# A graph layer on one core: node features as 64-row columns, 16-bit column lists made once, column copies in two of five groups, batch maxima in the other 64 partitions

## The chip, the core and the metric

One core of a Trainium2 chip runs the kernel. Its engines are named as in the profile: PE (matrix), DVE (vector), ACT (scalar), POOL and SP; each takes its instructions in order, and they wait for one another with semaphores. DMA queues are filled by SP, ACT and POOL. The metric is device time in microseconds (us). The kernel before took 3988.75, 3981.80 and 3985.86 us in three runs, a median of 3985.86.

## The reference

`x` holds 12500 nodes of 64 features. There are 412,500 edges (sender `src`, receiver `dst`, 32 edge features), sorted by receiver. Cut to what matters:

```python
h = relu(layernorm(x))
z = concat([h[src], h[dst], edge])                  # 64 + 64 + 32
messages = silu(z @ W1 + b1) @ W2 + b2
logits   = silu(z @ Wa1 + ba1) @ Wa2 + ba2
att      = softmax(logits, axis=0)                  # over all edges
agg      = segment_sum(messages * att, dst)
out      = x + silu(concat([h, agg]) @ Wu1 + bu1) @ Wu2 + bu2
```

The first products split into a part of the sender's node, one of the receiver's and one of the edge, so the parts of the nodes are made once for each node.

## The kernel before, in words

**Tiles.** The nodes are padded to NP = 12544, in 98 blocks of 128. The edges stand in columns of 128; K = 8 columns are a group, and NG = 403 groups make the main loop. A column's first layer is 128 wide: 64 of the message and 64 of the attention logit.

**The node stage** takes the layer norm of `x` in chunks, transposes it (`hT`: two blocks of nodes stacked on 128 partitions, so a node's 64 features are in the lower or in the upper half of a column), and makes two tables in DRAM: `ts_d` with the sender's part (stores L274 on SP's queue) and `tr_d` with the receiver's (stores L310 on ACT's queue). The last store of the stage, L313, puts `hT` itself into DRAM.

**The main loop** (L738) does for each group `load(g + 2)`, `begin(g)` and `end(g)`, with the sums of an earlier group in between:
- `load`: POOL issues one indirect DMA for each column (L533), which gathers 128 rows of `ts_d` into one of seven `gs` buffers; SP loads the window of receivers, the edge features and the receivers' numbers; DVE compares the numbers (L558), and PE multiplies (L562) into the PSUM tile `pe`.
- `begin`: DVE adds `gs` and `pe` (L573), ACT takes the tanh of the sum (L576).
- `end` and after: DVE makes the messages' activations and logits (L586 to L597), PE sums them by node (L646), and DVE adds the sums into the table `sums` (L671, L675).

**The softmax** goes by batches of groups with a running maximum. `put` also notes for each node the maximum of its batch, in the table `stand` (L678), which is laid out like `sums`: 128 partitions, of which 64 belong to one half of the nodes and 64 to the other, and one value repeated over the 64.

**Chosen groups.** Every third group, from 10 to 388, is chosen (127 of 403). In these the eighth column isn't gathered. Instead ACT copies its 128 columns of `hT` one by one into the tile `cols` (L504), each from a place whose number stands in a register (loads L500), and PE multiplies `cols` with the sender's weights (L568). Before that, SP loads the senders' numbers of the column to all partitions (`numbers`, L478), DVE turns them into column numbers with six operations (`places`, L487 to L493), and one more (L567) clears the half of each copied column that belongs to the other node. `burst` spreads the copies over six slots, two in each of the three groups before.

**The end** (L869 to L888). When the last group is summed, 13 tiles of 8 blocks (the last of 2) go through `factor` (ACT, the exponential of a batch's maximum, from `stand` into PSUM, L830), `first` (DVE, L838, and POOL, L843), `silu` (ACT's tanh, L848, and DVE, L849), `second` (PE, 4 matmuls in 8 passes, L856) and `rest` (DVE, L862, and the store of the output by SP, L864). The tiles take the three PSUM buffers of `acts_ps` in turn: `factor(t)` writes buffer t % 3, and the tanh of the same tile overwrites it. The loop's body is `first(t)`, `factor(t + 1)`, `silu(t - 1)`, `second(t - 1)`, `rest(t - 2)`; the engines' queues are then put in an order by a scheduler, except where `pin` keeps the order of the program.

A second path, `general`, is there for inputs whose receivers don't fit the windows. It doesn't run on these inputs.

Of the kernel before, what the change touches and what calls it, by code (L numbers as in the profile page):

```python
# [44 lines left out]
F32 = mybir.dt.float32  # L45
I32 = mybir.dt.int32
AF = mybir.ActivationFunctionType
# [6 lines left out]
P = 128  # L54
# [19 lines left out]
EVERY = 3  # L74
PHASE = 1
SLOTS = (((0, 24), (24, 24)), ((48, 24), (72, 12)), ((84, 24), (108, 20)))
# [4 lines left out]
BIG = 3.0e38  # L81


PARTS = [("pair", 4 * C), ("we", C), ("bias", C), ("wu2h", 2 * D), ("wa2", U), ("bu2", D), ("w_bu", U),
         ("w2b", U), ("wu1a", U), ("wu2", D), ("ba2", 1), ("w_bup", 2 * U), ("bu1", 1)]
# [5 lines left out]
def gnn_kernel(ctx: ExitStack, tc: tile.TileContext, n_edges, x, src, src_row, dst, dst_row, first, edge,  # L91
# [14 lines left out]
    hT_d = dram.tile([2 * D, NB // 2, P], F32, name="hT_d")  # L106
# [19 lines left out]
    w_bu = part["w_bu"][:D + 1]  # L126
# [29 lines left out]
    hT = const.tile([2 * D, NB // 2, P], F32, name="hT")  # L156
# [8 lines left out]
    with tc.tile_pool(name="node1", bufs=1) as node1, \  # L165
# [7 lines left out]
        for c, n in chunks:  # L173
            xc = node.tile([P, CB, D], F32, name="xc", bufs=min(len(chunks), 8))[:, :n, :]
# [138 lines left out]
        pin(nc.scalar.dma_start(hT_d, hT))  # L313
# [6 lines left out]


def node_bias(tc, b, v, work, ps):

    nc = tc.nc
    NB, w_bu = v["NB"], v["w_bu"]
    n = min(4, NB - b)
    hb = work.tile([D + 1, 4, P], F32, name="hb")
    nc.vector.memset(hb[D:, :, :], 1.0)
    for r in range(2):
        nc.sync.dma_start(hb[:D, r:n:2, :], v["hT_d"][r * D:(r + 1) * D, b // 2:(b + n) // 2, :])  # L330
    pb = ps.tile([P, 4, P], F32, name="mt")
    nc.tensor.matmul(pb[:U, :n, :], w_bu, hb[:, :n, :], start=True, stop=True)
    return pb[:U, :n, :]
# [60 lines left out]
def one_pass(tc, n_edges, v):  # L394
# [17 lines left out]
    with ExitStack() as ctx:  # L412
# [5 lines left out]
        stand = keep.tile([P, NH + 2 * W], F32, name="stand")  # L418
# [15 lines left out]
        nc.vector.memset(start[:, 1:2], BIG)  # L434
# [5 lines left out]
        hT = v["hT"].rearrange("d b p -> d (b p)")  # L440
        stack = keep.tile([2 * D, C], F32, name="stack")
        nc.vector.tensor_tensor(stack, v["w_pair"][:, 0, :C], v["w_pair"][:, 0, C:], ALU.add)
        half = keep.tile([P, 1], F32, name="half")
        nc.vector.memset(half[:D], 0.0)
        nc.vector.memset(half[D:], 1.0)
# [10 lines left out]
        with tc.tile_pool(name="work2", bufs=2) as work2, \  # L456
# [3 lines left out]
            pes, gss, lgs, ps_, psums, sps, pps, ees, mts, nums, cols = ({} for _ in range(11))  # L460
# [10 lines left out]

            chosen = {g for g in range(8, NG - 12) if g % EVERY == PHASE}

            def numbers(g):
                if g in chosen:
                    e = (g * K + K - 1) * EP
                    n = nums[g] = small.tile([P, EP], I32, name="num", bufs=2)
                    nc.sync.dma_start(n, bass.AP(tensor=v["src_row"].tensor,  # L478
                                                 offset=v["src_row"][:, e:].offset, ap=[[0, P], [1, EP]]))

            def places(g):
                if g not in chosen:
                    return
                n = nums[g]
                near = small.tile([1, EP], F32, name="near", bufs=1)
                to = small.tile([1, EP], I32, name="to", bufs=2)
                pin(nc.vector.tensor_scalar(to, n[0:1], 1, None, op0=ALU.logical_shift_right))  # L487
                m = NB // 2
                pin(nc.vector.tensor_scalar(near, to, 1.0 / m, 0.5 / m - 0.5, op0=ALU.mult, op1=ALU.add))
                pin(nc.vector.tensor_scalar(near, near, ROUND, None, op0=ALU.add))  # L490
                pin(nc.vector.tensor_scalar(near, near, ROUND, float(1 - m * P), op0=ALU.subtract, op1=ALU.mult))
                pin(nc.vector.scalar_tensor_tensor(to, to, float(P), near, op0=ALU.mult, op1=ALU.add))
                pin(nc.vector.tensor_scalar(n, n, 1, None, op0=ALU.bitwise_and))  # L493
                cols[g] = small.tile([P, EP], F32, name="cols", bufs=2), to

            def columns(g, first, n):
                if g not in chosen:
                    return
                to, at = cols[g]
                _, regs = nc.values_load_multi_w_load_instructions(  # L500
                    at[0:1, first:first + n], engines=[ENG.Activation], min_val=0, max_val=NP // 2 - 1,
                    skip_runtime_bounds_check_because=WHY)
                for i in range(n):
                    pin(nc.scalar.copy(to[:, first + i:first + i + 1], hT[:, bass.ds(regs[i], 1)]))  # L504
# [19 lines left out]
            def load(g):  # L524
# [40 lines left out]
                if g in chosen:  # L565
                    to, _ = cols[g]
                    pin(nc.vector.scalar_tensor_tensor(to, nums[g], half, to, op0=ALU.is_equal, op1=ALU.mult))  # L567
                    pin(nc.tensor.matmul(pe[:, K - 1, :], to, stack, start=False, stop=True))  # L568
# [91 lines left out]
            def put(g, part=None):  # L660

                if g % NQ == 0 and g not in at_lo:
                    registers(g, ENG.DVE, at_lo, base_lo, NH + W)
                    registers(g, ENG.DVE, at_hi, base_hi, NH + W)
                s = batch[g]
                for h, at in enumerate((at_lo, at_hi)):
                    rows, cols = slice(h * U, (h + 1) * U), bass.ds(at[g], W)
                    if part != "stand":
                        pp = pps[g]
                        if g == starts[s]:  # L670
                            pin(nc.vector.scalar_tensor_tensor(sums[rows, cols], sums[rows, cols],  # L671
                                                               scale[rows, s:s + 1], pp[rows],
                                                               op0=ALU.mult, op1=ALU.add))
                        else:
                            pin(nc.vector.tensor_tensor(sums[rows, cols], sums[rows, cols], pp[rows],  # L675
                                                        ALU.add))
                    if part != "sums":
                        pin(nc.vector.tensor_copy(stand[rows, cols],  # L678
                                                  nmax[rows, s + 1:s + 2].to_broadcast([U, W])))
# [8 lines left out]
            def inputs(t):  # L688

                n = P // 2 * NC  # L690
                if t < 8:
                    i = (t // 4 + (NG - 1) // NQ + 1) % 2
                    bs[t], xs[t] = eos[i][:, t % 4 * n:(t % 4 + 1) * n], hT[:, t * n:(t + 1) * n]
# [40 lines left out]

            for g in range(AHEAD):
                load(g)
            done = 0
            for g in range(NG):  # L738
# [9 lines left out]
                if g < 4:  # L748
                    w = -(-(NH + 2 * W) // 4)
                    for k, table in enumerate((sums, stand)):  # L750
                        piece = table[:, g * w:min((g + 1) * w, NH + 2 * W)]
                        pin(nc.scalar.activation(
                            piece, start[:, k:k + 1].to_broadcast([P, piece.shape[1]]), AF.Copy))
# [5 lines left out]
                numbers(g + 7)  # L759
                places(g + 6)  # L760
# [57 lines left out]
            free.append(hT[:, 8 * P // 2 * NC:8 * P // 2 * NC + K * C])  # L818
# [6 lines left out]
            def factor(t):  # L825
                n = width(t)
                if t in (1, 2):
                    acts_ps.append(one_ps.tile([P, 4, P], F32, name=(None, "sp", "mt")[t]).rearrange("p k c -> p (k c)"))
                fac = facs[t] = acts_ps[t % 3][:, :P // 2 * n]
                pin(nc.scalar.activation(fac.rearrange("u (p b) -> u p b", b=n),  # L830
                                         fv[:, :, t * NC:t * NC + n], AF.Exp, bias=last, scale=-1.0))
# [59 lines left out]
def general(tc, n_edges, v, dst):  # L891
# [7 lines left out]
    with ExitStack() as ctx:  # L899
# [11 lines left out]
        dst_sb = keep.tile([EP, T], I32, name="dst_g")  # L911
# [14 lines left out]
        with tc.tile_pool(name="bu_g", bufs=2) as work, \  # L926
                tc.tile_pool(name="bu_g_ps", bufs=2, space=PSUM) as bu_ps:
            for b in range(0, NB, 4):
                n = min(4, NB - b)
                bu = work.tile([U, 4, P], F32, name="bu_g")[:, :n, :]  # L930
                nc.scalar.copy(bu, node_bias(tc, b, v, work, bu_ps))
                nc.sync.dma_start(bu_d[:, b:b + n, :], bu)
# [142 lines left out]
def _laid_out(w):  # L1075
# [17 lines left out]
    part["w_bu"][:D + 1] = np.concatenate([w["Wu1"][:D], w["bu1"][None]])  # L1093
# [47 lines left out]
```

## Time and profile before

| | |
|---|---|
| runs | 3988.75, 3981.80, 3985.86 us |
| profiled execution | 3986.92 us, of which its span is 3985.1 us |
| mean granted clock of PE | 0.64 |
| HBM traffic | 360.42 MB read, 25.72 MB written |

A row of the page's fifth part reads: line, engine, operation, output <- inputs, count, then busy us and mean ns of one, then the engine's idle time just before and what ended most of it. A row of a timeline reads: start in us from the start of the span, us, engine, line, operation, and in brackets the idle time before and its releaser. "x8" in such a row is eight instructions in a row, put together.

### The profile page before, as it was taken

How to read it: one execution, taken by the hardware profiler on the slowest of the kernel's cores; microseconds unless marked ns; L12 is line 12 of the kernel's file. 1: busy time of each engine (PE TensorE's matmuls, PEld its weight loads, DVE VectorE, ACT ScalarE, POOL GpSimd, SP SyncE). 2: the span in 40 equal slices, each digit the busy share in tenths (PEclk: the TensorE clock that was granted, in tenths of full speed). 3: DMA queues.
4: the chain of work that ended last, by engine and by line, in shares of the span. 5: the costliest groups of instructions: out<-in, count | busy, mean ns of one | idle time of the engine just before them, and what ended most of it. 6: DMA issues, size and time to landing. Idle time of an engine off the chain costs nothing. (4 is left out here: it accounts for less than half of the span.)

```text
span 3985.1 us, 80416 instructions
## 1 busy us (share of the span) xinstructions
PE 2332.9 (59%) x11238; PEld 1888.3 (47%) x11238; DVE 3264.8 (82%) x9553; ACT 2173.0 (55%) x17477; POOL 2950.2 (74%) x3122
## 2 busy tenths in 40 slices
PE   6556566666666555555555555555655555555566
PEld 5444444454444444444444444444544444444455
DVE  6888888888888787888878888887878887878787
ACT  3655555555555555555555555555555555555512
POOL 3777777777777777777777777777777777777774
PEclk8766666666666666666666666666666665666666
DMA  8333343333333333333333333333333333333333
GB/s 287 101 99 99 95 110 92 103 99 102 102 92 95 93 85 93 87 92 88 89 94 84 95 93 86 94 84 94 88 91 94 84 95 87 91 95 84 104 105 85
DMA packets 219778, 391.64 MB, mean 98 GB/s; under 512 B 72209, under 2 KB 146898, under 8 KB 206050
## 3 DMA queue, kind: packets, MB, share of 16 engines
q0 software_dynamic: 99104, 203.16, 19.1%
q1 hardware_dynamic: 118754, 173.60, 16.7%
q10 hardware_dynamic: 1376, 9.67, 0.6%
q14 instruction: 452, 3.70, 0.3%
q8 instruction: 92, 1.51, 0.2%
HBM read 360.42 MB, written 25.72 MB: 97 GB/s over the span
## 5 line engine op out<-in xcount | busy, mean ns | idle before, releaser
L533 POOL DMA_INDIRECT gs<-ts_d,src_sb x3097 | 2933.0, 947 | 992.6 <-issue 854.1
L562 PE MATMUL pe<-wins,eo 128*128 128x256 f32 x3224 | 1465.1, 630 | 925.7 <-DVE eo L558 679.6
L504 ACT COPY cols<-hT 128x1 f32 x16256 | 1605.0, 187 | 717.7 <-issue 714.8
L562 PEld LDWEIGHTS pe<-wins,eo 128*128 128x128 f32 x3224 | 970.9, 318 | 1222.7 <-DVE eo L558 769.0
L576 ACT ACTIVATE pe<-gs 128x1024 f32<-128x1024 f32 x403 | 413.7, 1026 | 928.6 <-DVE gs L573 496.8
L573 DVE TENSOR_TENSOR gs<-pe,gs 128x1024 f32<-128x1024 f32 (+1 forms) x403 | 475.4, 1180 | 393.6 <-DMA gs<-ts_d,src_sb 369.2
L640 DVE TENSOR_SCALAR wt<-iota_w,dloc,p 128x40 f32<-128x40 f32 x3224 | 726.1, 321 | 1.8
L646 PE MATMUL sp<-wt,acts 128*65 128x40 f32 x6448 | 628.8, 268 | 6.3 <-DVE wt L640 3.9
L646 PEld LDWEIGHTS sp<-wt,acts 128*65 128x65 f32 x6448 | 589.9, 183 | 16.2 <-DVE wt L640 9.7
L657 PEld LDWEIGHTS mt<-ss,w2u 65*128 65x128 f32 x806 | 203.0, 279 | 336.2 <-issue 173.9
L657 PE MATMUL mt<-ss,w2u 65*128 65x40 f32 x806 | 181.6, 319 | 242.3 <-DVE gm L623 202.0
L616 PE MATMUL mt<-ident,mx 128*128 128x128 f32 x107 | 47.4, 443 | 445.8 <-DVE sums L675 427.2
L594 DVE TENSOR_TENSOR pe<-pe,w_all 128x512 f32<-128x512 f32 x403 | 281.8, 699 | 13.4
L558 DVE TENSOR_SCALAR eo<-dbs,bj 64x256 f32<-64x256 int32 x806 | 277.9, 375 | 18.2 <-DMA dbs<-in_dst_row_dram 9.0
L592 DVE SCALAR_TENSOR_TENSOR pe<-pe,gs 128x512 f32<-128x512 f32 x403 | 280.3, 696 | 10.5
L586 DVE SCALAR_TENSOR_TENSOR acts<-pe,gs 128x512 f32<-128x512 f32 x403 | 277.2, 688 | 12.4 <-ACT pe L576 3.2
L597 DVE TENSOR_REDUCE lg<-pe 128x8 f32<-128x512 f32 x403 | 277.0, 687 | 10.5
L616 PEld LDWEIGHTS mt<-ident,mx 128*128 128x128 f32 x107 | 19.5, 182 | 456.9 <-issue 455.0
L678 DVE COPY stand<-nmax 64x40 f32 x806 | 161.0, 200 | 3.2
L671 DVE SCALAR_TENSOR_TENSOR sums<-sums,scale,mt 64x40 f32 x214 | 54.2, 253 | 89.2 <-PE mt L657 85.0
L675 DVE TENSOR_TENSOR sums<-sums,mt 64x40 f32 x592 | 111.5, 188 | 4.7 <-PE mt L657 0.6
L357 DVE TENSOR_SCALAR bu<-mt,w_all 64x256 f32<-64x256 f32 (+1 forms) x50 | 23.9, 477 | 88.7 <-PE mt L348 88.3
(124 smaller groups left out, 1062.7 us busy)
## 6 DMA issues: line engine op xcount, KB each, us to landing
eo<-in_edge_dram SPq DMA_DIRECT2D x100, 512.0 KB
dbs<-in_dst_row_dram SPq DMA_DIRECT2D x200, 256.0 KB
gs<-ts_d,src_sb POOLq DMA_INDIRECT x3097
wins<-tr_d SPq DMA_DIRECT2D x806, 32.0 KB
num<-in_src_row_dram SPq DMA_DIRECT2D x127, 64.0 KB
ts_d<-ts SPq DMA_DIRECT2D x5, 896.0 KB
tr_d<-tr ACTq DMA_DIRECT2D x5, 896.0 KB
hT_d<-hT ACTq DMA_DIRECT2D x1, 3136.0 KB
```

The source lines that it names most:

```text
L504: pin(nc.scalar.copy(to[:, first + i:first + i + 1], hT[:, bass.ds(regs[i], 1)]))
L533: nc.gpsimd.indirect_dma_start(out=full[:rows, j, :], out_offset=None, in_=ts_d[:, :], in_offset=bass.IndirectOffsetOnAxis(ap=src_full[:ro ...
L558: pin(nc.vector.tensor_scalar(eo[:WR, e], db[:, e], bj[g // NQ % 2 * WR:(g // NQ % 2 + 1) * WR, g, h:h + 1], None, op0=ALU.is_equal))
L562: pin(nc.tensor.matmul(pe[:, 2 * q:2 * q + 2, :], eo[:, q * EP:(q + 1) * EP], win[:, q // 2, :, :], start=True, stop=q < H - 1 or g not in ...
L573: pin(nc.vector.tensor_tensor(gss[g][:, :n, :], pes[g][:, :n, :], gss[g][:, :n, :], ALU.add))
L576: pin(nc.scalar.activation(pes[g], gss[g], AF.Tanh))
L586: pin(nc.vector.scalar_tensor_tensor(acts[g % ACTS][:, :, 0:U], th[:, :, U:C], 1.0, gs[:, :, U:C], op0=ALU.add, op1=ALU.mult))
L592: pin(nc.vector.scalar_tensor_tensor(att, th[:, :, 0:U], 1.0, gs[:, :, 0:U], op0=ALU.add, op1=ALU.mult))
L594: pin(nc.vector.tensor_tensor(att, att, wa2[:EP, None, :].to_broadcast([EP, K, U]), ALU.mult))
L640: pin(nc.vector.tensor_scalar(wt[:, j, :], iota_w[:EP, j // H, :], dloc[:, g * K + j:g * K + j + 1], p[:, k + j:k + j + 1], op0=ALU.is_equ ...
L646: pin(nc.tensor.matmul(sp, acts[g % ACTS][:, j, :], wt[:, j, :], start=j == 0, stop=j == K - 1))
L657: pin(nc.tensor.matmul(pp, w2u.rearrange("s h u -> s (h u)"), sps.pop(g), start=True, stop=True))
```

## The change

- **Chosen groups**: from 10 to 390, those with g % 5 of 0 or 3, 153 of 403. The copies of one chosen group have five slots of 32 or 24 columns, one for each half group, beginning 9 or 10 half groups ahead.
- **One column a node**: the new tile `hS` holds `hT` in its first NP/2 columns. Its other columns hold, on partitions 0 to 63, a copy of the upper half of `hT` (`upper`: four DMAs inside SBUF on SP's queue, 64 x 1568 floats each), so that each node is one column on partitions 0 to 63. `cols` has 64 partitions, the mask of L567 goes, and the matmul contracts over 64 rows (`w_s`). The chunks of `x` are loaded into parts of `hS` first.
- **Lists**: `column_lists` works out the column numbers of all chosen groups at once, 7 DVE operations for each of the two residues, and stores them in DRAM as 16-bit numbers; `listed` loads one line of 128 of them for each chosen group. `numbers` and `places` go, and with them the 127 loads of numbers.
- **Batch maxima**: `stand` is now the other half of `hS`, partitions 64 to 127 and columns from NP/2: 32 rows for each half of the nodes. In `factor`, a matmul with the 0/1 matrix `pick` spreads the two values over 64 partitions each, into PSUM, and the exponential then works in place.
- The store of `hT` in DRAM goes, and with it `node_bias`, which only `general` used.

```diff
-EVERY = 3
-PHASE = 1
-SLOTS = (((0, 24), (24, 24)), ((48, 24), (72, 12)), ((84, 24), (108, 20)))
+EVERY = 5
+LEADS = {0: 9, 3: 10}
+SLOTS = ((0, 32), (32, 24), (56, 24), (80, 24), (104, 24))
+FIRST = 10
...
-        pin(nc.scalar.dma_start(hT_d, hT))
...
-        stand = keep.tile([P, NH + 2 * W], F32, name="stand")
+        stand = v["hS"][D:, NH:]
...
+        w_s = v["w_pair"][:D, 0, :C]
+        pick = keep.tile([P, P], F32, name="pick")
+        nc.vector.memset(pick, 0.0)
+        for h in range(2):
+            nc.vector.memset(pick[D + R * h:D + R * h + 1, h * U:(h + 1) * U], 1.0)
...
-            chosen = {g for g in range(8, NG - 12) if g % EVERY == PHASE}
+            chosen = [g for g in range(FIRST, NG - 12) if g % EVERY in LEADS]
+            of_phase = {r: [g for g in chosen if g % EVERY == r] for r in LEADS}
...
+            def column_lists():
+                m = NB // 2
+                for i, (r, gs) in enumerate(of_phase.items()):
+                    n, e = len(gs), (gs[0] * K + K - 1) * EP
+                    num = small.tile([P, EP], I32, name="num", bufs=2)[:n]
+                    nc.sync.dma_start(num, bass.AP(tensor=v["src_row"].tensor, ...
...
+                    pin(nc.vector.scalar_tensor_tensor(column, num, float(NH), near, op0=ALU.mult, op1=ALU.add))
+                    nc.sync.dma_start(v["list_d"][i, :n, :], column)
+
+            def upper(k, n):
+                w = -(-NH // n)
+                a, b = k * w, min((k + 1) * w, NH)
+                nc.sync.dma_start(hS[:D, NH + a:NH + b], hS[D:, a:b])
+
+            def listed(g):
                 if g in chosen:
...
+                    to = lists[g] = small.tile([1, EP], U16, name="listed", bufs=3)
+                    nc.sync.dma_start(to, v["list_d"][list(LEADS).index(g % EVERY),
+                                                      (g - of_phase[g % EVERY][0]) // EVERY][None, :])
...
             def columns(g, first, n):
...
+                if first == 0:
+                    cols[g] = small.tile([D, EP], F32, name="cols", bufs=2)
...
-                    pin(nc.scalar.copy(to[:, first + i:first + i + 1], hT[:, bass.ds(regs[i], 1)]))
+                    pin(nc.scalar.copy(cols[g][:, first + i:first + i + 1], hS[:D, bass.ds(regs[i], 1)]))
...
             def burst(g, k):
-                for i in range(EVERY):
-                    columns(g + 3 + i, *SLOTS[EVERY - 1 - i][k])
+                for c in range(g, g + 7):
+                    if c in chosen and 0 <= 2 * g + k - (2 * c - LEADS[c % EVERY]) < len(SLOTS):
+                        columns(c, *SLOTS[2 * g + k - (2 * c - LEADS[c % EVERY])])
...
                 if g in chosen:
-                    to, _ = cols[g]
-                    pin(nc.vector.scalar_tensor_tensor(to, nums[g], half, to, op0=ALU.is_equal, op1=ALU.mult))
-                    pin(nc.tensor.matmul(pe[:, K - 1, :], to, stack, start=False, stop=True))
+                    pin(nc.tensor.matmul(pe[:, K - 1, :], cols.pop(g), w_s, start=False, stop=True))
...
+            column_lists()
             for g in range(AHEAD):
                 load(g)
...
+                    upper(g, 4)
...
-                numbers(g + 7)
-                places(g + 6)
+                listed(g + 7)
...
                 fac = facs[t] = acts_ps[t % 3][:, :P // 2 * n]
-                pin(nc.scalar.activation(fac.rearrange("u (p b) -> u p b", b=n),
-                                         fv[:, :, t * NC:t * NC + n], AF.Exp, bias=last, scale=-1.0))
+                pin(nc.tensor.matmul(fac.rearrange("u (p b) -> u p b", b=n), pick[D:],
+                                     fv[:, :, t * NC:t * NC + n], start=True, stop=True))
+                pin(nc.scalar.activation(fac, fac, AF.Exp, bias=last, scale=-1.0))
```

As the program stands after the change, `upper` has its four DMAs in SP's queue between the last stores of `ts_d`, three of them ahead of the last one; in the end of the kernel PE's order is ones, pick 0, the last projection, pick 1, pick 2, second 0, pick 3, second 1, pick 4 and so on, and ACT's is exp 0, exp 1, exp 2, tanh 0, exp 3, tanh 1, exp 4 and so on.

More of the change, by code (lines that the diff above doesn't have):

```diff
@@ L46 @@
 I32 = mybir.dt.int32
+U16 = mybir.dt.uint16
 AF = mybir.ActivationFunctionType
@@ L105, in gnn_kernel @@
     tr_d = dram.tile([NP + WR, C], F32, name="tr_d")
-    hT_d = dram.tile([2 * D, NB // 2, P], F32, name="hT_d")
+    list_d = dram.tile([len(LEADS), P, EP], U16, name="list_d")
     bu_d = dram.tile([U, NB, P], F32, name="bu_d")
@@ L172, in gnn_kernel @@
         xcs = []
-        for c, n in chunks:
-            xc = node.tile([P, CB, D], F32, name="xc", bufs=min(len(chunks), 8))[:, :n, :]
+        room = hS.shape[1] - NP // 2
+        for i, (c, n) in enumerate(chunks):
+            at = NP // 2 + i * CB * D
+            if (i + 1) * CB * D <= room:
+                xc = hS[:, at:at + n * D].rearrange("p (b d) -> p b d", d=D)
+            else:
+                xc = node.tile([P, CB, D], F32, name="xc", bufs=1)[:, :n, :]
             nc.sync.dma_start(xc, x_v[:, c:c + n, :])
@@ L319, in gnn_kernel @@
         general(tc, n_edges, locals(), dst[:EP])
[L322 to L333, printed above, removed]
 def tile_bias(tc, c, first, v, work, ps, bus):
@@ L439, in one_pass @@
         dbs = keep.tile([P, NQ * H * P], F32, name="dbs")
[L440 to L445, printed above, removed]
+        hS = v["hS"]
+        w_s = v["w_pair"][:D, 0, :C]
[3 more added lines that the diff above has]
+            nc.vector.memset(pick[D + R * h:D + R * h + 1, h * U:(h + 1) * U], 1.0)
         w2u = keep.tile([S1, 2, U], F32, name="w2u")
@@ L459, in one_pass @@
                 tc.tile_pool(name="one_ps", bufs=1, space=PSUM) as one_ps:
-            pes, gss, lgs, ps_, psums, sps, pps, ees, mts, nums, cols = ({} for _ in range(11))
+            pes, gss, lgs, ps_, psums, sps, pps, ees, mts, lists, cols = ({} for _ in range(11))
             w2t_ps = one_ps.tile([P, 4, P], F32, name="mt")[:U, 0, :S1]
@@ L481, in places @@
[L481 to L494, printed above, removed]
+            chosen = [g for g in range(FIRST, NG - 12) if g % EVERY in LEADS]
@@ L496, in columns @@
             def columns(g, first, n):
-                if g not in chosen:
-                    return
-                to, at = cols[g]
+                if first == 0:
+                    cols[g] = small.tile([D, EP], F32, name="cols", bufs=2)
                 _, regs = nc.values_load_multi_w_load_instructions(
-                    at[0:1, first:first + n], engines=[ENG.Activation], min_val=0, max_val=NP // 2 - 1,
+                    lists[g][0:1, first:first + n], engines=[ENG.Activation], min_val=0, max_val=NP - 1,
@@ L924, in general @@
                 nc.scalar.dma_start(flat[:, b * S1:b * S1 + n], zero[:, :n])
[L926 to L932, printed above, removed]
+        with tc.tile_pool(name="bu_g", bufs=2) as work:
+            for t in range(v["NT"]):
+                m = min(NC, NB - t * NC)
+                raw = work.tile([U, 2, P // 2 * NC], F32, name="raw_g")
+                for h in range(2):
+                    nc.sync.dma_start(raw[:, h, :P // 2 * m], v["bq_d"][t, h * U:(h + 1) * U, :P // 2 * m])
+                bu = work.tile([U, NC, P], F32, name="bu_g")[:, :m, :]
+                for h in range(2):
+                    for k in range(2):
+                        nc.scalar.copy(
+                            bu[:, k * m // 2:(k + 1) * m // 2, h * P // 2:(h + 1) * P // 2],
+                            raw[:, h, k * P // 4 * m:(k + 1) * P // 4 * m].rearrange(
+                                "u (p i) -> u i p", i=m // 2))
+                nc.sync.dma_start(bu_d[:, t * NC:t * NC + m, :], bu)
         with tc.tile_pool(name="gather_g", bufs=2) as gather, \
```

48 lines of the change are left out of this document (28 added, 20 removed).

## The prediction

> **What bounds the kernel now.** I read the page first (busy time, costliest groups), then the waits and the timeline of POOL, one stretch of the steady loop, the start, and the end.
>
> ```profile
> span 3985.1 us, 80416 instructions
> ...
> PE 2332.9 (59%) x11238; PEld 1888.3 (47%) x11238; DVE 3264.8 (82%) x9553; ACT 2173.0 (55%) x17477; POOL 2950.2 (74%) x3122
> ...
> L533 POOL DMA_INDIRECT gs<-ts_d,src_sb x3097 | 2933.0, 947 | 992.6 <-issue 854.1
> ```
>
> DVE has the largest share, yet POOL is the pace: its 3097 gathers, and what stands before each of them, fill nearly the whole span. The waits (us in total, times, longest) and the timeline of POOL:
>
> ```profile
> POOL gs L533 <- issue: 854.1, 2802, 0.3
> POOL gs L533 <- DMA ts_d<-ts: 47.4, 1, 47.4
> POOL gs L533 <- DMA gs<-ts_d,src_sb: 46.9, 149, 1.8
> ```
> ```profile
> 49.82 1.10 POOL L533 DMA_INDIRECT gs<-ts_d,src_sb  x1 [47.43 <-DMA ts_d<-ts]
> ...
> 85.34 0.94 POOL L533 DMA_INDIRECT gs<-ts_d,src_sb  x1 [1.81 <-DMA gs<-ts_d,src_sb]
> ...
> 2000.77 0.94 POOL L533 DMA_INDIRECT gs<-ts_d,src_sb  x1 [0.30 <-issue]
> 2002.02 0.94 POOL L533 DMA_INDIRECT gs<-ts_d,src_sb  x1 [0.30 <-issue]
> ...
> 3927.03 0.94 POOL L533 DMA_INDIRECT gs<-ts_d,src_sb  x1 [0.30 <-issue]
> ```
>
> Once the sender table has landed (47.43 us of waiting), POOL stops once for 1.81 us; no other gap before a gather is above 0.3 us. From the first start to the last it makes 3096 steps in 3927.03 - 49.82 = 3877.2 us, 1.252 us each. So the run is a start of 49.8 us, the gathers, and 3985.1 - 3928.0 = 57.1 us behind the last one. The profiled execution took 3986.92 us (its span and 1.8 us around it), 1.1 us above the median of the runs, 3985.86.
>
> **The steady loop.** The steps between two gathers in a row are 1.25 us: the 1000 us below hold 800 gathers. (Columns: the stretch and its length, busy us and instructions of PE, its weight loads, DVE, ACT and POOL, then the granted clock of PE, the DMA share and GB/s.)
>
> ```profile
> 2000.00:3000.00 1000.00, 578.39 (x2803) 471.30 (x2804) 815.23 (x2421) 569.25 (x4725) 756.47 (x800) 0.63 0.35 90
> ```
>
> The chosen groups rise from 127 to 153, so 26 gathers go: 26 x 1.25 = -32.5 us (by the mean step of the whole run it would be 32.6). That is only true while POOL stays the pace. Per five groups it then has 38 gathers, 47.5 us. What the others have in the same time:
>
> ```profile
> 1999.01 1.03 ACT L576 ACTIVATE pe<-gs 128x1024 f32<-128x1024 f32 x1 [2.09 <-DVE gs L573]
> 1999.98 0.18 ACT L652 COPY ss<-sp 65x40 f32<-65x40 f32 x1
> 2000.72 2.32 ACT L504 COPY cols<-hT 128x1 f32 x24 [0.57 <-issue]
> 2003.78 1.21 ACT L504 COPY cols<-hT 128x1 f32 x12 [0.73 <-issue]
> ```
> ```profile
> ACT cols L504 <- issue: 195.3, 274, 1.7
> ```
>
> ACT: 24 copies in 2.32 us is 0.097 each. Two chosen groups make 256 copies, 24.8 us; five tanh and five copies of `ss` are 5 x 1.21 = 6.1; the issue waits of the copies (the register loads) are 195.3 us in the same 1000 us, which are 800/23 = 34.8 chosen groups of before, 5.6 each, so 11.2 for two; about 1 for the small exponentials. That is 43.1 of 47.5 us. Each half group has one slot after the change, and ACT becomes the pace only if a slot, of ten in five groups, costs 0.44 us more than this. The copies are 64 partitions high instead of 128; no row has that form, and I take the same price (a shorter column of the same width has no reason to be dearer; a saving here would change nothing, as ACT isn't the pace). DVE loses six operations on the column numbers and one mask per chosen group:
>
> ```profile
> L567 DVE SCALAR_TENSOR_TENSOR cols<-num,half,cols 128x128 f32<-128x128 int32 x127 | 43.6, 343 | 2.0
> ...
> L493 DVE TENSOR_SCALAR num<-num 128x128 int32<-128x128 int32 x127 | 27.4, 216 | 0.0
> ```
>
> These are the dearest and the cheapest of seven, so 190 to 305 us of busy time leave DVE. By the POOL rows above this is worth nothing: POOL doesn't wait for DVE. It also pays for what is added there: the 26 extra `gs` copies of chosen groups, and 14 operations that make both lists once. The `listed` load of 256 B replaces a 64 KB one on SP's queue, two groups ahead of its first use, and the 64-row matmul on the copied columns replaces a 128-row one. Cover for all of this is the seven `gs` buffers (seven groups of 7 or 8 gathers, some 66 us); without it a late slot would show on POOL as a wait for a DMA or for DVE.
>
> **The start.** SP's queue gets four copies inside SBUF (`upper`, 64 x 1568 floats, 0.40 MB each). Three stand ahead of the last stores of the sender table, for which the first gather waits; the 3.1 MB store of `hT_d` on ACT's queue goes.
>
> ```profile
> 25.49 0.42 SPq L478 DMA_DIRECT2D num<-in_src_row_dram  x1
> ...
> 37.59 9.06 SPq L274 DMA_DIRECT2D ts_d<-ts  x4
> ```
> ```profile
> 10.00:20.00 10.00, 6.40 (x22) 4.76 (x23) 9.56 (x13) 4.48 (x8) 0.00 (x0) 1.00 1.03 431
> ...
> 40.00:50.00 10.00, 9.90 (x48) 8.41 (x48) 9.72 (x14) 4.08 (x9) 0.18 (x1) 1.00 0.66 265
> ...
> 80.00:90.00 10.00, 0.00 (x0) 0.00 (x0) 1.14 (x4) 0.00 (x0) 6.58 (x7) 0.50 1.02 237
> ```
>
> No copy inside SBUF is in this trace. At 431 GB/s one takes 0.9 us of the DMA engines, and these stand at a share of 0.66 while the table is stored, so the delay is from 0 (they fit into the spare third) to 4 us (all three in the way, each with an issue like the 0.42 above: 3 x 1.35). I take +0.5, near the lower end, since the stores follow PE, which is busy 9.9 of 10 us there. The 1.81 us stop falls at a DMA share of 1.02, with the `hT_d` store under way; without it the stop may go: -0.9, from -1.8 to 0.
>
> **The end.** Here the change adds a link. The batch maxima now stand in half the rows, and `factor(t)` gets a matmul (128x512, `pick`) that spreads them into PSUM ahead of its exponential. Three PSUM buffers serve all tiles in turn, so pick(k+3) needs what DVE's L849 of tile k has read. In the order of the engines PE does second(k), then pick(k+3); ACT does exp(k+3), then tanh(k+1). Before, second(k) ran beside exp(k+3):
>
> ```profile
> 3948.70 0.60 ACT L848 ACTIVATE pe<-gs 128x512 f32<-128x512 f32 x1 [1.71 <-POOL gs L843]
> ...
> 3955.26 0.60 ACT L848 ACTIVATE pe<-gs 128x512 f32<-128x512 f32 x1
> 3955.90 0.69 DVE L849 SCALAR_TENSOR_TENSOR gs<-pe,gs 128x512 f32<-128x512 f32 x1
> ...
> 3956.62 0.69 ACT L830 ACTIVATE pe<-stand,nmax 128x512 f32<-128x512 f32 x1 [0.76 <-DVE gs L849]
> 3956.64 1.48 PEld L856 LDWEIGHTS pe<-w_all,gs 128*128 128x128 f32 x6 [0.22 <-DVE gs L849]
> ...
> 3957.25 0.59 ACT L848 ACTIVATE sp<-gs 128x512 f32<-128x512 f32 x1
> ...
> 3958.78 1.94 PEld L856 LDWEIGHTS pe<-w_all,gs 128*128 128x128 f32 x8 [0.20 <-DVE gs L849]
> 3958.92 0.69 DVE L862 TENSOR_TENSOR gs<-pe,hT 128x512 f32<-128x512 f32 x1 [0.19 <-PE pe L856]
> ...
> 3970.43 0.60 ACT L848 ACTIVATE sp<-gs 128x512 f32<-128x512 f32 x1 [0.28 <-POOL gs L843]
> ```
>
> The first and the eleventh tanh are 21.73 us apart, 2.17 a tile. Now a tile is a chain: tanh to L849 0.64 (3955.26 to 3955.90), L849 to second 0.74, second to the next free PE 2.14 (3956.64 to 3958.78), pick, 0.19 from PE to its reader, exp to tanh 0.63 (3956.62 to 3957.25). Together 4.34 and pick. Its price hangs on the clock:
>
> ```profile
> 2009.37 3.78 PE L562 MATMUL pe<-wins,eo 128*128 128x256 f32 x8 [4.18 <-DVE eo L558]
> ...
> 132.34 1.97 PE L562 MATMUL pe<-wins,eo 128*128 128x256 f32 x8 [1.29 <-issue]
> ```
> ```profile
> 3945.00:3950.00 5.00, 0.62 (x2) 0.47 (x2) 2.83 (x8) 1.29 (x2) 2.48 (x2) 0.50 0.01 2
> ...
> 3960.00:3965.00 5.00, 4.84 (x20) 4.46 (x20) 4.90 (x10) 2.75 (x5) 2.73 (x3) 0.84 0.46 107
> ```
>
> Eight passes of 256 columns take 3.78 us or 1.97; two passes of 512 are half of that, 1.89 slow or 0.99 fast. No matmul over strided columns of `stand` is in the trace; ACT reads the same strides in 0.69 against 0.60 for a plain tile, so I add nothing. At the loop's mean granted clock of 0.63, read as 1.0 for 26% and 0.5 for the rest, pick is 1.65 and the tile 6.0 us. Nine such tiles, and one of 128 columns (a quarter of the pick, some 0.3 less exponential: 4.5), are 58.5; less 21.7 is +36.8. The first tanh stands behind three picks and the third exp instead of POOL: +1, from 0 to 2.7. After the eleventh tanh all is as before. So +37.8, from +30.2 (fast: 9 x 5.33 + 4.3 - 21.7) to +41.6 (slow: 9 x 6.23 + 4.5 - 21.7 + 2.7).
>
> The Trainium skill ("TensorE: Matmul & The Clock Gate", Part 1) says that a PE busy through one window of about 3.4 us is granted the full clock afterwards. By that rule the pick would cost its fast price, and the time would be that of the warm rival below; this trace grants 0.50 to 0.84 in the rows above, though PE is busy 4.84 of 5 us in the later one, and so goes against it in part.
>
> **The sum.** -32.5 - 0.9 + 0.5 + 37.8 = +4.9 us on the profiled 3986.92, and as much on the median: 3991, from -32.5 - 1.8 + 0 + 30.2 = -4.1 (3982) to -32.5 + 0 + 4 + 41.6 = +13.1 (3999). A change under 0.2%, 8 us, is about what a measurement of this kernel can't tell from none.
>
> **The rivals.**
> - The end stays warm. A chain of picks at the fast price: -32.5 - 0.9 + 0.5 + 30.2 = -2.7, 3983. For it: a clock of 0.84 in one stretch. Against it: PE will rest about 2.2 of each 6 us, more than it does now.
> - The end stays cold, and the start is late; this is the case that is slower: the upper end of the sum, +13, 3999. For it: 0.50 in the first stretch of the end, and the new rests of PE. It decides as soon as a tile takes about 6.2 us and the copies delay the table by over 2.
> - The picks are hidden: PE is free when they are due, or the other two buffers carry the chain over. Then only the first tanh moves, up to 2.7: -32.5 - 0.9 + 0.5 + 2.7 = -30, 3956. For it: the exponentials were hidden before. Against it: exp(k+3) stands ahead of tanh(k+1) on ACT, so a late pick holds the next tile whatever else is free.
> - ACT becomes the pace: with 1 us more for each slot than in the rows above, 10 - 4.4 = 5.6 us per five groups, 76 times, is 426, and +5 beside it: about 4417. The margin of 0.44 is small, but the copies and loads are those of the rows.
> - The change doesn't do what it says: fewer gathers, but DVE's groups (815 of 1000 us busy) set the same pace. Then -0.9 + 0.5 + 37.8 = +37, 4023. Against it: POOL never waits over 0.3 us, and DVE loses work.
>
> **How the numbers follow.** Forecast 0.44; warm 0.13; cold 0.24; hidden 0.10; ACT 0.05; no gain in the loop 0.04. Time 3991, the likeliest case's sum. The range 3977 to 4000 holds forecast, warm and cold with the spread of the runs (3.5 us to each side of their middle) and leaves 0.19 outside. Faster: hidden and 0.04 of warm, 0.14. Same: forecast and the rest of warm, 0.53. Slower: cold, ACT, no gain, 0.33.
>
> **What would show it.** POOL: 3071 gathers at 1.25 us, first one at about 50.3, last end near 3896; no stop of 1.81 us. ACT: copies in bursts of 24 and 32, tanh still released by DVE's `gs`. The end: two passes of 128x512 on PE per tile, tanh to tanh near 6.0 us instead of 2.17, exp released by PE, and 95 us behind the last gather instead of 57. I am wrong if tanh to tanh stays below 4 us, or if gathers wait for more than 0.3 us in the loop.

## The result, and the profile after

The changed kernel took 6554.98 us (median of 4, 6553.71 to 6558.06), the kernel before 3986.05: 1.6448 times as long (95% interval 1.6419 to 1.6476), 2569 us more. The forecast was 3991.

The page of the changed kernel, its busy times and four of its costliest groups:

```profile
span 6556.3 us, 86323 instructions
...
PE 2729.1 (42%) x11316; PEld 2084.4 (32%) x11316; DVE 3115.8 (48%) x8704; ACT 2472.1 (38%) x20805; POOL 2919.7 (45%) x3096
...
L538 POOL DMA_INDIRECT gs<-ts_d,src_sb x3071 | 2902.5, 945 | 3510.4 <-issue 3451.6
L508 ACT COPY cols<-hS 64x1 f32 x19584 | 1918.6, 187 | 3782.1 <-issue 3782.1
...
L589 DVE SCALAR_TENSOR_TENSOR acts<-pe,gs 128x512 f32<-128x512 f32 x403 | 278.5, 691 | 2335.1 <-ACT pe L579 2331.9
...
L579 ACT ACTIVATE pe<-gs 128x1024 f32<-128x1024 f32 x403 | 411.9, 1022 | 112.9 <-DVE gs L576 63.8
```

The gathers cost what they did (945 ns), but POOL now stands idle for 3510 us. No engine is busy for half of the span. The groups that tell why are the copies (L504 before, L508 now) and the tanh (L576 before, L579 now). Before, their rows were:

```profile
L504 ACT COPY cols<-hT 128x1 f32 x16256 | 1605.0, 187 | 717.7 <-issue 714.8
L576 ACT ACTIVATE pe<-gs 128x1024 f32<-128x1024 f32 x403 | 413.7, 1026 | 928.6 <-DVE gs L573 496.8
```

The idle time just before the copies went from 717.7 to 3782.1 us, all of it now "issue", in which ACT waits for nothing that this view shows. ACT's tanh hardly waits for DVE any more (496.8 us before, 63.8 now), and DVE waits 2331.9 us for the tanh. So ACT is the pace, though its busy share fell from 55% to 38%. Its timeline:

```profile
3000.38 3.06 ACT L508 COPY cols<-hS 64x1 f32 x32 [5.79 <-issue]
3008.39 2.32 ACT L508 COPY cols<-hS 64x1 f32 x24 [4.96 <-issue]
3011.13 1.03 ACT L579 ACTIVATE pe<-gs 128x1024 f32<-128x1024 f32 x1 [0.41 <-issue]
3012.09 0.18 ACT L655 COPY ss<-sp 65x40 f32<-65x40 f32 x1
3016.42 2.32 ACT L508 COPY cols<-hS 64x1 f32 x24 [4.15 <-issue]
```

A slot of 24 copies still takes 2.32 us. Ahead of each stand 4 to 6 us instead of 0.6 to 0.7: the load of the column numbers into registers. A load isn't in the busy time, but it has a row in the view of its source line (on the engine's queue, ACTq; the three figures are the shortest, median and longest in ns, then come the starts of the first and the last in us). First the kernel before, then the changed one:

```profile
L500 ACTq TENSOR_LOAD <-to x762: 781/1485/1693, 120.6 to 3766.4; - x191
```
```profile
L504 ACTq TENSOR_LOAD <-listed x765: 5012/5055/7262, 93.9 to 6321.8; - x192
```

About as many loads, the median one of 24 numbers in both, at 3.4 times the price. The sum closes with it. Per five groups the prediction had 43.1 us for ACT, 11.2 of it for the waits before copies; these are now 3782.1 us over 153 / 2 = 76.5 such fives, 49.4 each, which makes 81.3. The steady loop agrees (columns as in the prediction; 467 gathers):

```profile
2000.00:3000.00 1000.00, 400.30 (x1669) 306.11 (x1669) 456.39 (x1283) 382.69 (x3304) 440.64 (x467) 0.55 0.19 51
```

38 gathers at 1000 / 467 us are 81.4 us. Before, five groups had 38.33 gathers on average, 47.9 us. 76.5 x (81.4 - 47.9) = 2563 of the 2571 us by which the spans differ.

### The profile page after: what moved, and what is told of

Read it like the earlier page. It is cut to its first block, busy times and chain, and to the rows that moved or that the text cites. A ratio compares the mean times of both kernels' runs of the same rounds, so it can differ in the third digit from the quotient of the medians.

```text
span 6556.3 us, 86323 instructions
## 1 busy us (share of the span) xinstructions
PE 2729.1 (42%) x11316; PEld 2084.4 (32%) x11316; DVE 3115.8 (48%) x8704; ACT 2472.1 (38%) x20805; POOL 2919.7 (45%) x3096
## 5 line engine op out<-in xcount | busy, mean ns | idle before, releaser
L538 POOL DMA_INDIRECT gs<-ts_d,src_sb x3071 | 2902.5, 945 | 3510.4 <-issue 3451.6
L508 ACT COPY cols<-hS 64x1 f32 x19584 | 1918.6, 187 | 3782.1 <-issue 3782.1
L567 PE MATMUL pe<-wins,eo 128*128 128x256 f32 x3224 | 1494.1, 643 | 653.1 <-DVE eo L563 437.0
L589 DVE SCALAR_TENSOR_TENSOR acts<-pe,gs 128x512 f32<-128x512 f32 x403 | 278.5, 691 | 2335.1 <-ACT pe L579 2331.9
L567 PEld LDWEIGHTS pe<-wins,eo 128*128 128x128 f32 x3224 | 1000.9, 327 | 954.6 <-DVE eo L563 508.7
L660 PE MATMUL mt<-ss,w2u 65*128 65x40 f32 x806 | 255.5, 417 | 2467.7 <-ACT ss L655 1619.9
L649 PE MATMUL sp<-wt,acts 128*65 128x40 f32 x6448 | 783.9, 308 | 2.9 <-DVE wt L643 2.9
L649 PEld LDWEIGHTS sp<-wt,acts 128*65 128x65 f32 x6448 | 751.5, 230 | 3.7 <-DVE wt L643 3.4
L576 DVE TENSOR_TENSOR gs<-pe,gs 128x1024 f32<-128x1024 f32 (+1 forms) x403 | 470.8, 1168 | 40.5 <-issue 25.1
L579 ACT ACTIVATE pe<-gs 128x1024 f32<-128x1024 f32 x403 | 411.9, 1022 | 112.9 <-DVE gs L576 63.8
L571 PE MATMUL pe<-w_all,cols 64*128 64x128 f32 x306 | 111.9, 463 | 352.8 <-ACT cols L508 352.8
L571 PEld LDWEIGHTS pe<-w_all,cols 64*128 64x128 f32 x306 | 70.6, 286 | 449.5 <-ACT cols L508 402.8
L681 DVE COPY hS<-nmax 32x40 f32 x806 | 168.6, 209 | 18.0
```

What stands on the lines that cost most here:

```text
L508: pin(nc.scalar.copy(cols[g][:, first + i:first + i + 1], hS[:D, bass.ds(regs[i], 1)]))
L538: nc.gpsimd.indirect_dma_start(out=full[:rows, j, :], out_offset=None, in_=ts_d[:, :], in_offset=bass.IndirectOffsetOnAxis(ap=src_full[:ro ...
L567: pin(nc.tensor.matmul(pe[:, 2 * q:2 * q + 2, :], eo[:, q * EP:(q + 1) * EP], win[:, q // 2, :, :], start=True, stop=q < H - 1 or g not in ...
L576: pin(nc.vector.tensor_tensor(gss[g][:, :n, :], pes[g][:, :n, :], gss[g][:, :n, :], ALU.add))
L579: pin(nc.scalar.activation(pes[g], gss[g], AF.Tanh))
L589: pin(nc.vector.scalar_tensor_tensor(acts[g % ACTS][:, :, 0:U], th[:, :, U:C], 1.0, gs[:, :, U:C], op0=ALU.add, op1=ALU.mult))
```

## The experiments

The first question was whether the width of the list is the cause, or another of the new things around the copies: a narrower copy from a wider tile, a list that a DMA brings, other slots. The second was what the rest of the change is worth once that is out of the way.

**e1: the list in 32 bits.**

```diff
-    list_d = dram.tile([len(LEADS), P, EP], U16, name="list_d")
+    list_d = dram.tile([len(LEADS), P, EP], I32, name="list_d")
...
-                    column = small.tile([P, EP], U16, name="column", bufs=2)[:n]
+                    column = small.tile([P, EP], I32, name="column", bufs=2)[:n]
...
-                    to = lists[g] = small.tile([1, EP], U16, name="listed", bufs=3)
+                    to = lists[g] = small.tile([1, EP], I32, name="listed", bufs=3)
```

> The changed kernel with one thing turned back: the list of column numbers is 32 bits wide (in DRAM, in the tile that DVE writes and in the loaded line); everything else stays. Theory A (ACT reads 16-bit numbers into registers one by one, about 0.19 us each: 3782 us of idle time before 19584 copies): the idle time before the copies falls to 550 to 860 us (0.7 to 1.1 for each of 765 loads), POOL is the pace again at 1.25 us a gather, and the time is 3975 to 4000, with the longer end of the kernel in it (about 6 us a tile). Rival B (the cost lies in what else is new: copies of 64 partitions from the wider tile, a list that a DMA brings, or the place of the slots): 6500 to 6600, idle time as before.

Measured: 3998.85 us (7 runs) beside 3987.81, a ratio of 1.0028 (1.0017 to 1.0040). From the page, the source line and the timeline of POOL of this kernel:

```profile
L508 ACT COPY cols<-hS 64x1 f32 x19584 | 1918.7, 187 | 898.5 <-issue 896.9 <-PE sp L649 1.6
```
```profile
L504 ACTq TENSOR_LOAD <-listed x765: 1472/1495/2583, 94.2 to 3757.4; - x192
```
```profile
52.05 1.10 POOL L538 DMA_INDIRECT gs<-ts_d,src_sb  x1 [49.66 <-issue]
...
3892.18 0.94 POOL L538 DMA_INDIRECT gs<-ts_d,src_sb  x1 [0.30 <-issue]
```

Three types turned back bring the time back by 2556 us. The load is 1.50 us again, and the idle time before the copies is 898.5 us, a little above the 550 to 860 expected. The row of the first gather names no releaser here. The 3071 gathers take (3892.18 - 52.05) / 3070 = 1.251 us each, and POOL is the pace. Copies of 64 partitions, a list from DRAM and the new slots are cleared. What is left, +11 us, is dealt with by e7 and e10.

**e2: the kernel before, with 16-bit numbers.**

```diff
-                pin(nc.vector.scalar_tensor_tensor(to, to, float(P), near, op0=ALU.mult, op1=ALU.add))
+                at = small.tile([1, EP], U16, name="at16", bufs=2)
+                pin(nc.vector.scalar_tensor_tensor(at, to, float(P), near, op0=ALU.mult, op1=ALU.add))
...
-                cols[g] = small.tile([P, EP], F32, name="cols", bufs=2), to
+                cols[g] = small.tile([P, EP], F32, name="cols", bufs=2), at
```

> The kernel before with one thing added: the last operation on the column numbers writes them as 16-bit numbers, still on DVE, for each chosen group. Theory A: 16256 numbers at 0.19 us are 3140 us of idle time before the copies; per three groups ACT then has 12.4 for copies, 24.7 for numbers, 3.6 for tanh and ss and about 1, 41.7 us against 28.7 of POOL: 5300 to 5700. Rival B: 3970 to 4010, as the kernel before.

Measured: 5534.09 us (one run), with the load of its source line at the new price:

```profile
L502 ACTq TENSOR_LOAD <-at x762: 2533/5019/5768, 122.1 to 5332.5; - x191
```

The one edit does it alone, in the kernel before, with numbers that DVE made on the spot.

**e3 and e4: each load halved, for 16-bit and for 32-bit lists.**

```diff
-                _, regs = nc.values_load_multi_w_load_instructions(
-                    lists[g][0:1, first:first + n], engines=[ENG.Activation], ...
+                regs = []
+                for b in range(0, n, n // 2):
+                    regs += nc.values_load_multi_w_load_instructions(
+                        lists[g][0:1, first + b:first + b + n // 2], engines=[ENG.Activation], ...
```

> The changed kernel, 16-bit lists kept, with two loads of registers for each slot, each of half the numbers (16 or 12). Theory A, priced by the number: the idle time before the copies stays within 10% of 3782, the time within 6450 to 6700. Theory A', priced by the load (about 4.9 us for each of 765): the idle time doubles to some 7500, the time goes to about 10300.

> The 32-bit list with two loads for each slot, each of half the numbers. If a 32-bit load costs by the load (0.7 us each), ACT gets 10 x 0.7 = 7 us more per five groups, 43.1 + 7 = 50.1 against 47.5 of POOL: about 2.6 x 76 = 200 us above the kernel with the 32-bit list and one load, 4150 to 4250. If it costs by the number, the time is the same as that one's (within 30 us).

Measured: 6655.69 us with the 16-bit list and 3999.09 with the 32-bit one (one run each). The loads of e3, then of e4:

```profile
L506 ACTq TENSOR_LOAD <-listed x1530: 2531/2552/3841, 94.9 to 6422.3; - x192
```
```profile
L506 ACTq TENSOR_LOAD <-listed x1530: 767/783/1620, 93.4 to 3757.1; - x192
```

Half the numbers, half the time, in both forms: 12 and 24 numbers take 2.55 and 5.06 us, or 0.78 and 1.50. So a load is priced by the number, 0.21 us in the one form and 0.06 in the other. For the 32-bit list I had expected a price by the load (4150 to 4250); that was wrong.

**e8, e9 and e12: is it the width?** In e8 the list has 32 bits, but the load reads only the lower half of each word; in e9 the load reads whole 32-bit words that lie eight bytes apart.

```diff
 e8, against e1
-                    lists[g][0:1, first:first + n], engines=[ENG.Activation], ...
+                    lists[g].bitcast(U16).rearrange("o (n t) -> o n t", t=2)[0:1, first:first + n, 0], ...
 e9 and e12, against e1
-                    to = lists[g] = small.tile([1, EP], I32, name="listed", bufs=3)
+                    to = lists[g] = small.tile([1, EP, 2], I32, name="listed", bufs=3)[:, :, 0]
```

> The 32-bit list, of which the register loads read only the lower 16 bits of each word: 16-bit numbers, four bytes apart and aligned. Theory (the width of what is read sets the price): 6450 to 6700, with 3600 to 3900 us idle before the copies. Rival (the price comes from two numbers packed into one word, half of them not aligned): 3990 to 4010.

> The 32-bit list with its numbers eight bytes apart in the loaded line. Theory (width): 3990 to 4010, idle time before the copies as with the plain 32-bit list, about 900. Rival (a row of words that lie side by side is fetched together, and what can't be is fetched one by one): 6000 or more, idle time above 3000.

> The kernel of e9 again: 32-bit numbers eight bytes apart in the loaded line. Theory of the row (only 32-bit words that lie side by side are fetched together, anything else one by one at 0.19 us): the time of the changed kernel, 6450 to 6700, with 3600 to 3900 us idle before the copies. Theory of the width: 3990 to 4010.

Measured: 7407.53 us (e8) and 7435.93 (e9) on a chip on which the kernel before itself took 6002.87 (more on it under e5), and 6559.77 (e12) beside 3986.81 on another, one run each. The loads of e8, then of e12:

```profile
L504 ACTq TENSOR_LOAD <-listed x765: 3595/5022/7272, 151.3 to 7132.7; - x192
```
```profile
L504 ACTq TENSOR_LOAD <-listed x765: 5021/5047/7260, 93.7 to 6323.7; - x192
```

e12 reads 32-bit numbers and is as slow as the changed kernel (6554.98). The times of e8 and e9 can't be compared with those of the other chip, but the price of a load can: the median of e9 is 5038 ns beside 5047 in e12, and that of a load of 32-bit words side by side is the same on both chips (1494 ns in e5, 1496 in e11). My theory of the width fell: the low price goes to 32-bit words that lie side by side, and 16-bit numbers, side by side or four bytes apart, and 32-bit words eight bytes apart all pay 0.21 us each. Why is not shown. Four neighbours cost 4 x 0.062 = 0.25 us, not far above the 0.21 of one alone, so neighbours may be fetched in fours; no run tried that.

**e5 and e11: the choice of groups alone.** The kernel before, with the new pattern and slots and three buffers for `num`, `to` and `cols`.

```diff
-EVERY = 3
-PHASE = 1
-SLOTS = (((0, 24), (24, 24)), ((48, 24), (72, 12)), ((84, 24), (108, 20)))
+EVERY = 5
+LEADS = {0: 9, 3: 10}
+SLOTS = ((0, 32), (32, 24), (56, 24), (80, 24), (104, 24))
+FIRST = 10
...
-            chosen = {g for g in range(8, NG - 12) if g % EVERY == PHASE}
+            chosen = [g for g in range(FIRST, NG - 12) if g % EVERY in LEADS]
...
```

> The kernel before with the new choice of groups alone: two of five, the five slots, three buffers for each of num, to and cols; 32-bit numbers made on DVE for each group, hT on 128 partitions, the mask, the batch maxima and the end as before. Theory: the 26 gathers are worth 32.5 us on the path of POOL and nothing else moves, 3950 to 3958 against a kernel before of 3986 to 3988. Rival: two of five is too much for ACT or DVE, and gathers wait: 3980 or more, with waits of POOL above 0.3 us in the loop.

> The kernel of e5 again (the kernel before with the new choice of groups alone). Theory: 26 gathers less on POOL's path and nothing else, 31 to 37 us below the kernel before of the same chip: 3950 to 3957 beside 3987. Rival: two of five is too much for ACT, gathers wait, 3980 or more.

Measured: e5 6198.57 us beside 6002.87 for the kernel before (1.0332, 1.0309 to 1.0354), e11 3961.25 beside 3986.81 (0.9935, 0.9919 to 0.9952). The timeline of ACT in e5:

```profile
1999.97 0.19 ACT L505 COPY cols<-hT 128x1 f32 x1 [1.24 <-issue]
2001.39 0.19 ACT L505 COPY cols<-hT 128x1 f32 x1 [1.23 <-issue]
2002.12 0.19 ACT L505 COPY cols<-hT 128x1 f32 x1 [0.55 <-issue]
...
2006.99 2.32 ACT L505 COPY cols<-hT 128x1 f32 x24 [1.46 <-issue]
```

On that chip many of the copies come singly, 0.5 to 1.2 us apart; the load of registers has its usual price there (median 1494 ns in e5). With that, more copies cost time whatever POOL does. e5 is therefore no test of the theory, and e11 is: the gathers are the path again, first and last of them here.

```profile
52.95 1.10 POOL L535 DMA_INDIRECT gs<-ts_d,src_sb  x1 [50.55 <-DMA ts_d<-ts]
...
3898.95 0.94 POOL L535 DMA_INDIRECT gs<-ts_d,src_sb  x1 [0.30 <-issue]
```

From first to last these are 3846.0 us instead of 3877.2: the 26 gathers bring 31.2 of the 32.5 expected. The whole is 25.6, so the time lies above the 3950 to 3957 expected: the first gather is 3.1 us later (three loads of numbers instead of two now stand among the stores of the sender table, which may be why), and some 5 us appear behind the last instruction (below).

**e7 and e10: the end, and the start.** Both have the 32-bit list. In e7 one step of the end moves; in e10 the copies inside SBUF also go to ACT's queue.

```diff
 e7 and e10, the loop of the end
                 if t < NT:
                     first(t)
-                if t + 1 < NT:
-                    factor(t + 1)
                 if 1 <= t <= NT:
                     silu(t - 1)
+                if t + 1 < NT:
+                    factor(t + 1)
+                if 1 <= t <= NT:
                     second(t - 1)
 e10, the node stage
         pin(nc.scalar.dma_start(tr_d[NP:, :], zero[:WR, :]))
+        for k in range(4):
+            w = NP // 8
+            pin(nc.scalar.dma_start(hS[:D, NP // 2 + k * w:NP // 2 + (k + 1) * w], hS[D:, k * w:(k + 1) * w]))
...
-                    upper(g, 4)
```

> The kernel with the 32-bit list, and in the loop of the end factor(t + 1) moved behind silu(t - 1) and ahead of second(t - 1), so that on ACT the tanh no longer stands behind an exponential that waits for a pick. Theory (the 6.23 us of a tile are a chain through the order of the engines): the chain now closes every two tiles, 0.64 + 0.74 + 2.16 + 2.1 + 0.66 + 0.9 (L844) + 1.27 (POOL) and hand-overs, about 8.7, or 4.3 a tile, PE's own 2.16 + 2.1 beside it: 19 us less, 3976 to 3984 where the 32-bit list alone gives 3999. Rival (the three PSUM buffers close the chain whatever the order): 6.2 us a tile still, 3995 to 4003.

> The 32-bit list, the order of the end as in e7, and the four copies inside SBUF moved from SP's queue, between the stores of the sender table, to ACT's, behind the stores of the receiver table. Theory (start: the copies delay the sender table by 2.2 us; end: a tile is 4.2 us instead of 6.23): first gather at 49.5 to 50.3 instead of 52.1, and 19 + 2 us less than e1's 3999, so 3974 to 3982, some 9 us below the kernel before. Rival for the start (the copies only share the DMA engines): first gather still near 52.

Measured: e7 6234.36 us beside 6002.87 (1.0382, 1.0362 to 1.0402), on the chip of e5, so its time can't be compared with e1's; e10 3976.06 beside 3986.81 (0.9972, 0.9962 to 0.9982), within the 3974 to 3982 expected. One tile of the end in e1:

```profile
3923.90 0.59 ACT L854 ACTIVATE sp<-gs 128x512 f32<-128x512 f32 x1
3924.53 0.69 DVE L855 SCALAR_TENSOR_TENSOR gs<-sp,gs 128x512 f32<-128x512 f32 x1 [4.76 <-ACT sp L854]
...
3925.27 1.94 PEld L862 LDWEIGHTS pe<-w_all,gs 128*128 128x128 f32 x8 [3.57 <-DVE gs L855]
...
3927.44 2.07 PE L835 MATMUL sp<-hS,pick 64*128 64x512 f32 x2
3929.55 0.66 ACT L837 ACTIVATE sp<-sp,nmax 128x512 f32<-128x512 f32 x1 [5.05 <-PE sp L835]
3930.13 0.59 ACT L854 ACTIVATE mt<-hS 128x512 f32<-128x512 f32 x1
```

It is the predicted chain link by link: tanh, L855, second, pick, exp, tanh, 6.23 us, and the exp waits 5.05 us for PE. In e10 the tanh no longer stands behind that exp:

```profile
3923.88 0.59 ACT L856 ACTIVATE mt<-hS 128x512 f32<-128x512 f32 x1
3927.46 0.66 ACT L839 ACTIVATE sp<-sp,nmax 128x512 f32<-128x512 f32 x1 [2.99 <-PE sp L837]
3928.04 0.59 ACT L856 ACTIVATE pe<-gs 128x512 f32<-128x512 f32 x1
```

A tile is 4.16 us (4.17 in e7), near the 2.17 of second and the 2.07 of pick that PE has to do for it; the rival of the three PSUM buffers falls. And the start, the first gather and the copies' place on ACT's queue:

```profile
50.00 1.10 POOL L541 DMA_INDIRECT gs<-ts_d,src_sb  x1 [47.60 <-DMA ts_d<-ts]
```
```profile
71.45 5.13 ACTq L322 DMA_DIRECT2D hS<-hS  x4
```

The first gather is 2.05 us earlier than in e1, so the copies were the delay. Whether by their place in SP's queue or by their share of the DMA engines, e10 doesn't tell: on ACT's queue they are issued only at 71.45 us, when the table has long landed, so both are gone. The share of the DMA engines speaks for the second at least in part: from 35 to 40 and from 40 to 45 us it was 0.75 and 0.61 in the kernel before, 0.99 and 0.97 in e1, and 0.67 and 0.61 in e10.

The version that beats both kernels by most is e11 (3961.25 us), which takes one part of the change and leaves the rest.

## Why the prediction was wrong

- **The bound, POOL at 1.25 us a gather:** right for the kernel before, for e1, e10 and e11. The gathers' term, -32.5 and -0.9 for the stop, measured 3840.1 - 3877.2 = -37.1 in e1, -33.5 in e10 and -31.2 in e11. In e1 no gather after the first waits for more than 0.3 us, so the 1.5 us that the stop was longer are gone, and a gather takes 946 ns instead of 947, which over 3071 of them is the other 3 us.
- **ACT's budget: the step that failed.** "the issue waits of the copies (the register loads) are 195.3 us in the same 1000 us" and "so 11.2 for two" carried the price of loads of 32-bit numbers over to a list of 16-bit ones. I named and priced the lower copies, which cost nothing new, and the list only as a smaller DMA; what reads it got the old price unasked. The term was 49.4 instead of 11.2 us per five groups, and with the 32-bit list of e1 it is 898.5 / 76.5 = 11.7: the price was right for the form that it came from. The load has a row of its own in the trace of before, 1485 ns for 24 numbers, which the prediction doesn't use, and no row of before showed 16 bits, so the form should have been bounded from both sides, as the copies inside SBUF were.
- **The rival "ACT becomes the pace":** the right mechanism, at a chance of 0.05 and with 1 us more a slot. No run came near its point of decision, 0.44 us a slot; the load of 24 numbers alone costs 3.57 us more (5055 - 1485 ns). With that price the rival's own sum, 10 x 3.57 - 4.4 = 31.3 us a five, 76 times, would have been +2380.
- **Start:** +0.5 taken, +2.2 in e1 and +2.65 in the changed kernel (first gather at 52.47), inside the bounds of 0 to 4. The reason for the low end, that the stores follow PE, did not hold: PE was busy for 3.84 of the 5 us from 40 to 45 in e1 and for 4.90 before. By which way the copies held the stores up stays open (see e10).
- **End:** the chain was right, and its sum at the slow price too, to the hundredth (6.23). The lower bound is a slip, 9 x 5.33 + 4.3 - 21.7 being 30.6 and not 30.2, which moves no conclusion. The share of full clock was wrong. Between the first tanh and the last long tile of e1:

```profile
3915.00:3975.00 60.00, 40.21 (x93) 22.31 (x91) 19.49 (x39) 12.44 (x21) 13.92 (x11) 0.50 0.15 35
```

The granted clock is 0.50 throughout. From the last gather's end to the last instruction e1 has 96.9 us instead of the 55.2 of before: +41.7, the upper bound of 41.6. In e10 the same view has PE busy for 39.25 of 40 us, and still 0.50:

```profile
3917.00:3957.00 40.00, 39.25 (x94) 22.44 (x93) 21.09 (x39) 11.99 (x21) 13.31 (x11) 0.50 0.24 55
```

The warm rival falls with it. The rule of the Trainium skill that a PE busy through one window of about 3.4 us is granted the full clock ("TensorE: Matmul & The Clock Gate", Part 1) does not hold in this stretch, as the profile counts PE's busy time. In the start of the same kernel, from 35 to 60 us, PE is as busy (5.00 of each 5 us) and its clock is 1.00; what makes the difference no run tried.

- **What no step had:** about 4.6 us behind the last instruction. The last memset of e1 ends at 3990.02 of 3996.5, that of the kernel before at 3983.21 of 3985.1:

```profile
3989.96 0.06 DVE L894 MEMSET hS<- 128x1 f32 x1
```
```profile
3983.15 0.06 DVE L888 MEMSET hT<- 128x1 f32 x1
```

With it e1 closes: +2.2 - 37.1 + 41.7 + 4.6 = +11.4, the difference of the spans. The gap is 6.0 to 7.3 us in each kernel with the new choice of groups, e11 among them, and 1.9 in e2, which has the old one. Its cause was not tried.

## What to carry to other kernels

A change of a type is a change of every instruction that reads it; list these, registers' loads among them, and price each by a row of its own. An engine that waits for nothing ("issue") may be loading registers, and the view of that source line has the price that the busy time leaves out. For lists of numbers that go into registers, 32-bit words side by side are worth their memory: 0.06 us a number against 0.21. And where two engines pass a buffer round, write down the order of each engine's queue: moving one step behind another took a tile from 6.23 to 4.16 us.

## What the runs showed of the hardware that I had not expected

The price of a register from a list in SBUF: 0.06 us for 32-bit words side by side, and 0.21 for 16-bit numbers and for 32-bit words eight bytes apart. It is the same for a list that DVE wrote (the kernel before and e2) and one that a DMA brought (e1 and the changed kernel). The Trainium skill ("Runtime: NRT & Kernel Launch", Instruction fetch mechanics) gives about 200 ns a register, even in bulk, for loads which its list of terms calls loads from HBM; these runs show about that figure for lists in SBUF in the dear forms, and less than a third of it for 32-bit words side by side.

On one chip ACT's copies came with pauses between them, and the kernel before took 6002.87 us there instead of 3986.81. In e11's kernel, run there as e5, ACT had 2624.0 us of issue waits before copies in 3247 pieces, and 875.0 in 1037 on the other chip. What was slow on that chip, these runs don't show.
